# A third buffer for gathered rows, a gather beside each product, and a sum moved behind a mask, in a two-layer graph kernel

## The chip, the cores and the metric

The kernel runs on one core of one Trainium2 chip, as one program with one launch. The metric is the device time of that core in microseconds (us), the median of several runs. Five runs of the kernel before gave 1269.19 us as the median (1265.02 to 1273.97).

A core has engines that run side by side, each through its own list of instructions in order: TensorE (PE in the profile; PEld is its weight load), VectorE (DVE), ScalarE (ACT), GpSimd (POOL) and SyncE (SP), which here only issues DMAs. They wait for each other through semaphores. An instruction that waits holds up all that stand behind it in the list of its engine.

## What is computed

Input are x, 2708 x 256, and a square matrix adj, 2708 x 2708, with about 0.3 % of entries not zero. Layer 0 is a graph layer with LayerNorm; layer 1 is a two-step propagation, with LayerNorm too:

```python
support = adj @ x
x = _layernorm(x + relu(concat([x, support], 1) @ weight + bias))

R = adj + eye(N);  R = R / R.sum(-1, keepdims=True)
Z = 0;  Xf = x;  Xa = x
for n in range(2):
    A = _top_p_attention(Xa, W1, W2, W3)
    Xf = R @ Xf
    Xa = A @ Xa
    Z = Z + Xf @ U1[n].T + Xa @ U2[n].T
x = _layernorm(x + _layernorm(x + Z))
```

`_top_p_attention` forms softmax(q kT) over all 2708 columns, keeps in each row the largest probabilities until their sum reaches 0.9 (of equal ones the first), sets the others to zero and divides by the sum of what is kept.

## The kernel before

**Blocks.** The 2708 rows are NB = 22 blocks of 128 rows (the last, EDGE, has 20). A block of attention is a 128 x 2708 tile of exponentials `e`; four such tiles `es` (a fifth in step 2) are in use in turn.

**Three stages.** Layer 0 runs first and keeps x1 in SBUF. Step 1 of the attention (the loop at L931 over t) follows, then step 2 (the loop at L1311 over `per`). The text calls one turn of the latter a pass.

**R is kept sparse.** For each block m of R, layer 0 names the columns of adj that have any entry in these rows: at most 896, as CC = 7 chunks of CW = 128. During step 1, `adj_gather` (L377) fetches those columns' blocks of adj, and `adj_store` packs them in DRAM (`adjc_d`, and the diagonal block in `own_d`). A product of R with a vector block is then 8 *units*, each one matmul of 128 x 256: seven over the gathered chunks (k = 0 to 6) and one over the block's own rows (k = 7). The row numbers are in `ix`.

**Gathered rows of y.** The right side of unit k is 128 rows of `yf_d` (first half, s = 0) or `v_d` (second half, s = 1), gathered by an indirect DMA that GpSimd issues: `y_load` (L742), seven for a product (L746). They land in `yg`, which has two slots, `m % 2`; each slot has eight parts, the eighth for the block's own rows, which SP loads (L762). The rows of `v_d` are completed by the first half's results (`r_out` stores to `v_d`, L806), so the gathers of the second half can't start before the last product of the first half is stored.

**Order of R's units.** `r_units(n)` (L765) issues the next n units. With the first unit of product m it calls `r_load(s, m + 1)`: SP loads the packed blocks of R (`a_load`, one of three buffers `adj`), GpSimd issues the seven gathers, SP loads the own rows. The last unit of a product starts a load of what is to be added (`v_load` or `za_load`), and puts `r_out` into `later`, which VectorE runs two turns of g on. The first two products' gathers are issued at the end of step 1 (`y_at`, L928).

The table `units` (L1294) says how many units a pass has: 16 (`first`) before the loop, then 8 and 8 in passes 0 and 1, 18 in each of passes 2 to 9, none in pass 10 and 16 in each of passes 11 to 21. A pass spreads them over six turns g.

**A pass of step 2.** Pass `per` works on several blocks at once: the exponentials of block per + 2 (ScalarE L871, L875, as logits from TensorE L534 come in, the last third at g = 3), two tries for the threshold of block per + 1 (ScalarE L1002, L1005, with small instructions L1008 to L1018 behind them), the search of candidates of block per (VectorE L1059, L1066), the end of the search and the mask of block per - 1 (VectorE: L1075 to L1119, mask L1124), and the product of block per - 2 with ya (TensorE transposes L561, ScalarE copies L563, TensorE L590). TensorE's order within a turn g is written out by hand. VectorE's is a generator, `vector_slots` (L1146), of which each g runs one slot; the last slot runs marks 2 and 3, `begin_search` of the block per + 2 between them (L879 to L884: the sum of the three parts of the exponentials' sum, its reciprocal, its negative and the first level), and then the mask.

**LayerNorm at the end.** `Final` and `final_slot` (L1260): rows that have all their parts (`ready`) are normalised in the next passes. `middle` runs at g = 0: ScalarE writes to one of four `spares` (L1228), GpSimd multiplies and adds (L1243, L1244), and VectorE takes the second statistics (L1218) at g = 4 of the same pass.

**Room.** `yg`, the spares and `x1_edge` (the last block's rows, for step 1) share one tile, `y_room`. `c.u1`, the matrices U1, is read by `u1_project` (L673) before step 1's loop, and in `general_path`, which runs only if a flag says that the fast path's assumptions failed.

Of the kernel before, what the change touches and what calls it, by code (L numbers as in the profile page):

```python
# [20 lines left out]
P = 128  # L21
# [18 lines left out]
ML = 16  # L40
CW, CC = 128, 7
EARLY = 12
AT = 96
# [19 lines left out]
def gnn_two_layer_kernel(ctx: ExitStack, tc: tile.TileContext, N, xT_d, x_d, adj_d, w0_d, b0_d,  # L63
# [24 lines left out]
    nc = tc.nc  # L88
    D = x_d.shape[1]
    DA = w1_d.shape[1]  # L90
    NB = (N + P - 1) // P
    DC = D // P
# [13 lines left out]

    c = Common()
    c.N, c.D, c.DA, c.NB, c.DC, c.KH, c.CHS, c.rows = N, D, DA, NB, DC, KH, CHS, rows
    c.adj_d, c.out_d = adj_d, out_d
# [21 lines left out]
    NF = 6 * NB + 4  # L131
# [28 lines left out]
def fast_path(ctx, tc, c, flags, fint, xT_d, x_d, w0_d, b0_d, w1_d, w2_d, w3_d, u1_d, u2_d, g_d, b_d):  # L160
# [351 lines left out]
    assert not weights  # L512
    lists.end()
    y_room = big.tile([P, DC * N], FP, tag="Y", name="yg")
    YW = 2 * (CC + 1) * D
    yg = y_room[:, :YW].rearrange("p (s c d) -> p s c d", s=2, d=D)
    spares = [y_room[:, YW + D * i:YW + D * (i + 1)] for i in range(4)]
    x1_edge = y_room[:, YW + 4 * D:YW + 5 * D]
    lists = Lists(ML, NB, flags[:, NF - 2:], yg[:, 1].rearrange("p c d -> p (c d)"))
    lists.turn()  # L520

    NL = len(KPS) // 2
# [216 lines left out]
    later = [[], []]  # L739
    ready = []  # L740

    def y_load(s, m):  # L742
        y = yg[:, m % 2]
        rows_d = (c.yf_d, c.v_d)[s].rearrange("p k d -> (p k) d")
        for i in range(CC):
            nc.gpsimd.indirect_dma_start(out=y[:CW, i, :], out_offset=None, in_=rows_d,  # L746
                                         in_offset=bass.IndirectOffsetOnAxis(ap=ix[:CW, m, i:i + 1], axis=0))
        y_in[s, m] = y

    def a_load(m):  # L750
        a = adjp.tile([P, KH, P], FP, tag="adj", name="adj_t")
        nc.sync.dma_start(out=a[:CW, :CC, :].rearrange("p c i -> p (c i)"), in_=c.adjc_d[m])
        nc.sync.dma_start(out=a[:rows(m), CC, :], in_=c.own_d[m, :rows(m), :])
        a_in[m] = a

    def r_load(s, m):
        if m not in a_in:
            a_load(m)
        if (s, m) not in y_in:
            y_load(s, m)  # L760
        y = y_in.pop((s, m))
        nc.sync.dma_start(out=y[:rows(m), CC, :], in_=(c.yf_d, c.v_d)[s][:rows(m), m, :])  # L762
        r_in[s, m] = a_in.pop(m), y

    def r_units(n):  # L765
        for _ in range(n):
            s, m = r_queue[0]
            p = rows(m)
            if not r_now:
                r_now[:] = [ps_misc(), 0]  # L770
                if m + 1 < NB:
                    r_load(s, m + 1)
            acc, k = r_now
            a, y = r_in[s, m]
            kw = CW if k < CC else p
            nc.tensor.matmul(acc[:p, :D], lhsT=a[:kw, k, :p], rhs=y[:kw, k, :], start=k == 0, stop=k == CC)  # L776
# [24 lines left out]
    def r_out(s, m, acc, base):  # L801
        p = rows(m)
        if s == 0:
            nc.vector.scalar_tensor_tensor(base[:p], acc[:p, :D], rinv[:p, m:m + 1], base[:p],
                                           op0=ALU.mult, op1=ALU.add)
            nc.sync.dma_start(out=c.v_d[:p, m, :], in_=base[:p])  # L806
            if m == NB - 1:
                r_load(1, 0)
        else:
            arrive(m, base, acc, rinv[:p, m:m + 1])  # L810

# [107 lines left out]
    for t in range(n_u, NB):  # L919
        u1_project(t)  # L920
    extract1(2)
    nc.vector.memset(x1_edge, 0.0)
    nc.vector.tensor_copy(x1_edge[AT:AT + rows(EDGE)], x1[:rows(EDGE), EDGE, :])
    ends = None

    at = {(m // 2, 3 * (m % 2) + 1): m for m in range(4)}
    at.update({(m - 2, 3): m for m in range(4, NB)})
    y_at = {(NB - 2, 2): 0, (NB - 2, 5): 1}  # L928
    stores = []
    blocks = {}  # L930
    for t in range(NB):  # L931
# [214 lines left out]
    def vector_slots(a, b, begin):  # L1146
# [47 lines left out]
        yield  # L1194

    new, finals, done = [], [], []
# [215 lines left out]
def general_path(ctx, tc, c):  # L1412
# [13 lines left out]
    work = ctx.enter_context(tc.tile_pool(name="gwork", bufs=2))  # L1426
    small = ctx.enter_context(tc.tile_pool(name="gsmall", bufs=4))
    ps = ctx.enter_context(tc.tile_pool(name="gps", bufs=2, space=PSUM))

    def ps_lg():  # L1430
        return ps.tile([P, CH], FP, tag="lg", name="lg")
# [339 lines left out]
```

## Time and profile before

| | us |
|---|---|
| median of five runs | 1269.19 |
| the profiled execution | 1266.74 |
| its span, first to last instruction | 1265.0 |
| first unit of R (L776) starts | 722.8 |
| last gather of yf_d starts | 938.7 |
| first gather of v_d starts | 953.9 |
| last gather of v_d starts | 1217.9 |

| engine | busy us | share of the span |
|---|---|---|
| TensorE | 1192.0 | 94 % |
| TensorE's weight loads | 901.2 | 71 % |
| VectorE | 971.5 | 77 % |
| ScalarE | 734.7 | 58 % |
| GpSimd | 634.0 | 50 % |

How to read it: the median is over several executions, and the profile is of one of them, so sums over the profile are made against 1265.0 us. Matmul records overlap (the next starts before the last ends), so a share of 94 % for TensorE doesn't mean that it is at its peak. A float32 matmul leaves two records (704 for the 352 units of R). A pass of step 2 is read most easily from the starts of the mask, L1124. In rows of a timeline, a bracket tells the idle time of the engine before the instruction and what ended it.

### The profile page before, as it was taken

How to read it: one execution, taken by the hardware profiler on the slowest of the kernel's cores; microseconds unless marked ns; L12 is line 12 of the kernel's file. 1: busy time of each engine (PE TensorE's matmuls, PEld its weight loads, DVE VectorE, ACT ScalarE, POOL GpSimd, SP SyncE). 2: the span in 40 equal slices, each digit the busy share in tenths (PEclk: the TensorE clock that was granted, in tenths of full speed). 3: DMA queues.
4: the chain of work that ended last, by engine and by line, in shares of the span. 5: the costliest groups of instructions: out<-in, count | busy, mean ns of one | idle time of the engine just before them, and what ended most of it. 6: DMA issues, size and time to landing. Idle time of an engine off the chain costs nothing.

```text
span 1265.0 us, 18701 instructions
## 1 busy us (share of the span) xinstructions
PE 1192.0 (94%) x5772; PEld 901.2 (71%) x5772; DVE 971.5 (77%) x3254; ACT 734.7 (58%) x1299; POOL 634.0 (50%) x596
## 2 busy tenths in 40 slices
PE   8999999999899999999998969999998999999884
PEld 6888878863477777777776737777766777777663
DVE  2455545875999998988851399887788999999886
ACT  2000110135566665666665499878879999999821
POOL 1000000004545542677765087787756888888850
PEclk9999999999899999999999989999999999999997
DMA  7475445434222220233333155656654645655551
GB/s 200 152 209 177 152 142 175 135 106 126 88 66 82 74 72 10 60 98 101 89 80 98 58 173 179 185 180 187 179 118 127 198 142 172 198 152 167 165 116 30
DMA packets 104248, 164.92 MB, mean 130 GB/s; under 512 B 20162, under 2 KB 76870, under 8 KB 104138
## 3 DMA queue, kind: packets, MB, share of 16 engines
q1 hardware_dynamic: 77852, 107.57, 26.5%
q0 software_dynamic: 20544, 51.17, 15.7%
q10 hardware_dynamic: 5742, 4.89, 1.4%
q8 instruction: 48, 0.79, 0.3%
q14 instruction: 62, 0.51, 0.1%
HBM read 129.66 MB, written 33.90 MB: 129 GB/s over the span
## 4 chain that ended last, share of the span: by engine, by line
PE 37%; DVE 8%; ACT 6%; DMA 6%; issue 2%; POOL 2%; POOLq 0%; ACTq 0%
PE acc L590 17%; PE misc L776 7%; PE lg L534 5%; PE tr L561 4%; DMA yg<-v_d,ix 3%; DMA yg<-yf_d,ix 3%; DVE e L1124 2%; PE acc L698 2%; ACT e L1002 2%; DVE w L1119 1%; ACT e L1005 1%; ACT e L871 1%; PE misc L726 1%; POOL yg L746 1%; DVE cand L1066 1%
## 5 line engine op out<-in xcount | busy, mean ns | idle before, releaser
L563 ACT COPY wT<-tr 128x512 f32<-128x512 f32 (+2 forms) x258 | 136.4, 536 | 203.7 <-PE tr L561 203.7
L746 POOL DMA_INDIRECT yg<-v_d,ix x154 | 194.1, 1261 | 59.7 <-issue 25.0
L590 PE MATMUL acc<-ya,wT 128*128 128x256 f32 x924 | 222.9, 383 | 0.0
L590 PE MATMUL acc<-x,wT 128*128 128x256 f32 x882 | 218.8, 389 | 0.0
L746 POOL DMA_INDIRECT yg<-yf_d,ix x154 | 189.2, 1229 | 48.3 <-issue 25.6
L274 PE MATMUL acc<-y,adj_t 128*128 128x257 f32 x924 | 204.4, 380 | 0.0
L776 PE MATMUL misc<-yg,adj_t 128*128 128x256 f32 (+1 forms) x704 | 186.2, 395 | 18.5 <-DMA yg<-yf_d,ix 7.7
L590 PEld LDWEIGHTS acc<-x,wT 128*128 128x128 f32 x882 | 160.3, 191 | 58.9 <-issue 25.5
L590 PEld LDWEIGHTS acc<-ya,wT 128*128 128x128 f32 x924 | 172.3, 191 | 37.9 <-issue 16.7
L274 PEld LDWEIGHTS acc<-y,adj_t 128*128 128x128 f32 x924 | 173.9, 190 | 26.6 <-issue 1.9
L384 POOL DMA_INDIRECT adj_t<-in_adj,ix x154 | 163.7, 1063 | 51.6 <-issue 43.9
L776 PEld LDWEIGHTS misc<-yg,adj_t 128*128 128x128 f32 (+1 forms) x704 | 122.4, 189 | 69.4 <-issue 20.6
L534 PE MATMUL lg<-k,q 64*128 64x512 f32 (+3 forms) x528 | 137.1, 596 | 20.8 <-ACT e L871 7.4
L561 PE MATMUL tr<-ident,e 128*128 128x128 f32 (+1 forms) x946 | 145.1, 272 | 6.3 <-ACT wT L563 4.6
L561 PEld LDWEIGHTS tr<-ident,e 128*128 128x128 f32 (+1 forms) x946 | 117.4, 141 | 39.3 <-ACT wT L563 8.6
L351 POOL DMA_DIRECT2D part_d<-e x1 | 0.6, 573 | 272.6 <-DVE e L350 272.6
L1002 ACT ACTIVATE e<-e,st 128x2708 f32<-128x2708 f32 (+1 forms) x43 | 113.6, 2641 | 0.1
L1005 ACT ACTIVATE e<-e,st 128x2708 f32<-128x2708 f32 (+1 forms) x42 | 111.0, 2642 | 0.1
L462 ACT COPY x1T<-tr 128x256 f32<-128x256 f32 (+1 forms) x22 | 8.0, 364 | 174.6 <-PE tr L461 174.6
L596 DVE MAX8 cand<-e 128x8 f32<-128x170 f32 (+1 forms) x352 | 86.2, 316 | 14.7 <-ACT e L541 14.5
L1066 DVE MAX8 cand<-w 128x8 f32<-128x170 f32 (+1 forms) x352 | 94.1, 321 | 0.0
L534 PEld LDWEIGHTS lg<-k,q 64*128 64x128 f32 (+1 forms) x528 | 39.1, 182 | 52.6 <-issue 20.2
(247 smaller groups left out, 1744.3 us busy)
## 6 DMA issues: line engine op xcount, KB each, us to landing
adj_t<-in_adj SPq DMA_DIRECT2D x42, 704.0 KB
adj_t<-adjc_d SPq DMA_DIRECT2D x44, 448.0 KB
adjc_d<-adj_t SPq DMA_DIRECT2D x22, 256.0 KB
base<-za_d SPq DMA_DIRECT2D x40, 128.0 KB
adjc_d<-adj_t SPq DMA_DIRECT2D x22, 192.0 KB
xt<-in_x ACTq DMA_DIRECT2D x21, 128.0 KB
x_d<-x SPq DMA_DIRECT2D x21, 128.0 KB
x1b_d<-xb SPq DMA_DIRECT2D x21, 128.0 KB
```

The lines of the kernel that those rows point to most:

```text
L274: nc.tensor.matmul(acc[:p, :n], lhsT=halves[k // KH][:, k % KH, :p], rhs=y[:, k, :n], start=k == 0, stop=stop and k == NB - 1)
L384: nc.gpsimd.indirect_dma_start(out=a[:CW, i, :], out_offset=None, in_=adj_rows, in_offset=bass.IndirectOffsetOnAxis(ap=ix[:CW, m, i:i + 1] ...
L534: nc.tensor.matmul(lg[:p, h, at:at + b - a], lhsT=q[o, t * P:t * P + p], rhs=keys[s][o, i, :b - a], start=True, stop=True)
L561: nc.tensor.transpose(tr[:, k % 4, :p], columns(e[:p], k), ident[:p, :p])
L563: nc.scalar.copy(wT[:, :len(ks), :p], tr[:, :len(ks), :p])
L590: nc.tensor.matmul(acc[:p, :D], lhsT=wT[:, k % 4, :p], rhs=part_y(y, k), start=k == 0, stop=k == NB - 1)
L596: nc.vector.max(dst[:p, i * 8:(i + 1) * 8], src[:p, i * step:i * step + w])
L746: nc.gpsimd.indirect_dma_start(out=y[:CW, i, :], out_offset=None, in_=rows_d, in_offset=bass.IndirectOffsetOnAxis(ap=ix[:CW, m, i:i + 1], ...
L776: nc.tensor.matmul(acc[:p, :D], lhsT=a[:kw, k, :p], rhs=y[:kw, k, :], start=k == 0, stop=k == CC)
L1002: nc.scalar.activation(scr[:b.p, :N], e, AF.Relu, bias=b.nz, scale=b.l[k], accum_out=b.relu)
L1005: nc.scalar.activation(scr[:b.p, :N], e, AF.Sign, bias=b.nz, scale=b.l[k], accum_out=b.sign)
L1066: nc.vector.max(b.cand[:p, 8 * i:8 * i + 8], low[:p, SEG2 * i:SEG2 * (i + 1)])
```

## The change

- `yg` has three slots of seven parts. The own rows go to two free parts of the tile that holds R's blocks.
- With the first unit of product m, `r_load` is called for m + 2. It no longer issues the gathers but puts them in a list, `to_gather`; each unit issues one of them ahead of its matmul.
- The gathers of the first three products are issued at the end of step 1, and so are the loads of R's blocks for the first two.
- The units: 24 ahead of the loop (`first`), 8 and 16 in passes 0 and 1, 16 in each of passes 2 to 9; none in pass 10 and 16 in passes 11 to 21 as before.
- When the first half is stored, the loads and gathers of the second half's first two products are issued, all fourteen gathers in a row.
- The spares and `x1_edge` move to `c.u1`, and `x1_edge` is written inside step 1's loop at t = 0. `general_path` loads U1 again.
- In the last slot of `vector_slots` the mask comes right after marks 2 and 3, and `begin_search` behind it.

```diff
@@ fast_path @@
-    YW = 2 * (CC + 1) * D
-    yg = y_room[:, :YW].rearrange("p (s c d) -> p s c d", s=2, d=D)
-    spares = [y_room[:, YW + D * i:YW + D * (i + 1)] for i in range(4)]
-    x1_edge = y_room[:, YW + 4 * D:YW + 5 * D]
+    YW = CC * D
+    yg = y_room[:, :3 * YW].rearrange("p (s c d) -> p s c d", s=3, d=D)
+    idle = [c.u1[:, j, i, :] for j in range(DC) for i in range(2)]
+    spares = list(idle)
+    x1_edge = idle[0]
...
+    def y_rows(s, m, i):
+        rows_d = (c.yf_d, c.v_d)[s].rearrange("p k d -> (p k) d")
+        nc.gpsimd.indirect_dma_start(out=yg[:CW, m % 3, i, :], out_offset=None, in_=rows_d,
+                                     in_offset=bass.IndirectOffsetOnAxis(ap=ix[:CW, m, i:i + 1], axis=0))
+
     def y_load(s, m):
-        y = yg[:, m % 2]
-        rows_d = (c.yf_d, c.v_d)[s].rearrange("p k d -> (p k) d")
         for i in range(CC):
-            nc.gpsimd.indirect_dma_start(out=y[:CW, i, :], out_offset=None, in_=rows_d,
-                                         in_offset=bass.IndirectOffsetOnAxis(ap=ix[:CW, m, i:i + 1], axis=0))
-        y_in[s, m] = y
+            y_rows(s, m, i)
+        y_in[s, m] = yg[:, m % 3]
...
-    def r_load(s, m):
+    to_gather = []
+
+    def r_load(s, m, by_unit=False):
         if m not in a_in:
             a_load(m)
         if (s, m) not in y_in:
-            y_load(s, m)
-        y = y_in.pop((s, m))
-        nc.sync.dma_start(out=y[:rows(m), CC, :], in_=(c.yf_d, c.v_d)[s][:rows(m), m, :])
-        r_in[s, m] = a_in.pop(m), y
+            if by_unit:
+                to_gather.extend((s, m, i) for i in range(CC))
+                y_in[s, m] = yg[:, m % 3]
+            else:
+                y_load(s, m)
+        a, y = a_in.pop(m), y_in.pop((s, m))
+        own = a[:, CC + 1:CC + 1 + D // P, :].rearrange("p c i -> p (c i)")
+        nc.sync.dma_start(out=own[:rows(m)], in_=(c.yf_d, c.v_d)[s][:rows(m), m, :])
+        r_in[s, m] = a, y, own
...
             if not r_now:
                 r_now[:] = [ps_misc(), 0]
-                if m + 1 < NB:
-                    r_load(s, m + 1)
+                if m + 2 < NB:
+                    r_load(s, m + 2, True)
+            if to_gather:
+                y_rows(*to_gather.pop(0))
...
             if m == NB - 1:
                 r_load(1, 0)
+                r_load(1, 1)
...
-    y_at = {(NB - 2, 2): 0, (NB - 2, 5): 1}
+    y_at = {(NB - 3, 5): 0, (NB - 2, 3): 1, (NB - 1, 1): 2}
...
+        if t == 0:
+            nc.vector.memset(x1_edge, 0.0)
+            nc.vector.tensor_copy(x1_edge[AT:AT + rows(EDGE)], x1[:rows(EDGE), EDGE, :])
...
-            if (t, g) == (NB - 1, 2):
-                a_load(0)
+            if t == NB - 1 and 1 < g < 4:
+                a_load(g - 2)
...
     r_load(0, 0)
+    r_load(0, 1)
...
@@ vector_slots @@
-        for i in (2, 3):
-            if b:
-                mark(b, i)
-            if begin:
-                next(begin)
+        if b:
+            mark(b, 2)
+            mark(b, 3)
+            mask(b)
         if begin:
             run_all(begin)
-        if b:
-            mask(b)
         yield
...
-    first = 2 * (CC + 1)
-    units = {0: CC + 1, 1: CC + 1}
+    first = 3 * (CC + 1)
+    units = {0: CC + 1, 1: 2 * (CC + 1)}
```

More of the change, by code (lines that the diff above doesn't have):

```diff
@@ L108, in gnn_two_layer_kernel @@
     c.N, c.D, c.DA, c.NB, c.DC, c.KH, c.CHS, c.rows = N, D, DA, NB, DC, KH, CHS, rows
-    c.adj_d, c.out_d = adj_d, out_d
+    c.adj_d, c.out_d, c.u1_d = adj_d, out_d, u1_d
     c.x1_d = dram.tile([N, D], FP, name="x1_d")
@@ L514, in fast_path @@
     y_room = big.tile([P, DC * N], FP, tag="Y", name="yg")
-    YW = 2 * (CC + 1) * D
-    yg = y_room[:, :YW].rearrange("p (s c d) -> p s c d", s=2, d=D)
-    spares = [y_room[:, YW + D * i:YW + D * (i + 1)] for i in range(4)]
-    x1_edge = y_room[:, YW + 4 * D:YW + 5 * D]
-    lists = Lists(ML, NB, flags[:, NF - 2:], yg[:, 1].rearrange("p c d -> p (c d)"))
+    YW = CC * D
[3 more added lines that the diff above has]
+    x1_edge = idle[0]
+    lists = Lists(ML, NB, flags[:, NF - 2:], y_room[:, YW:])
     lists.turn()
@@ L770, in r_units @@
                 r_now[:] = [ps_misc(), 0]
-                if m + 1 < NB:
-                    r_load(s, m + 1)
+                if m + 2 < NB:
+                    r_load(s, m + 2, True)
+            if to_gather:
+                y_rows(*to_gather.pop(0))
             acc, k = r_now
-            a, y = r_in[s, m]
+            a, y, own = r_in[s, m]
             kw = CW if k < CC else p
-            nc.tensor.matmul(acc[:p, :D], lhsT=a[:kw, k, :p], rhs=y[:kw, k, :], start=k == 0, stop=k == CC)
+            nc.tensor.matmul(acc[:p, :D], lhsT=a[:kw, k, :p], rhs=y[:kw, k, :] if k < CC else own[:p],
+                             start=k == 0, stop=k == CC)
             r_now[1] += 1
@@ L921, in fast_path @@
     extract1(2)
-    nc.vector.memset(x1_edge, 0.0)
-    nc.vector.tensor_copy(x1_edge[AT:AT + rows(EDGE)], x1[:rows(EDGE), EDGE, :])
     ends = None
@@ L1428, in general_path @@
     ps = ctx.enter_context(tc.tile_pool(name="gps", bufs=2, space=PSUM))
+    for s in range(2):
+        nc.sync.dma_start(out=u1[:, :, s, :], in_=c.u1_d[s].rearrange("(c p) e -> p c e", p=P))
     def ps_lg():
```

## The prediction

> **What bounds the kernel now.** I read the page first, then busy time by stretches one pass of step 2's loop long, then the timelines of GpSimd, VectorE and TensorE inside passes, and last the table of waits. The page's part 1 suggests TensorE and nothing else:
>
> ```profile
> PE 1192.0 (94%) x5772; PEld 901.2 (71%) x5772; DVE 971.5 (77%) x3254; ACT 734.7 (58%) x1299; POOL 634.0 (50%) x596
> ```
>
> The share hides that in step 2 (from about 722 us on) GpSimd never stops. In its timeline a gather (L746) takes 0.95 us and the next starts 0.30 us later, so 1.25 us each. Twice a pass one is stretched:
>
> ```profile
> 869.62 3.71 POOL L746 DMA_INDIRECT yg<-yf_d,ix  x1 [0.30 <-PE misc L776]
> 873.63 0.95 POOL L746 DMA_INDIRECT yg<-yf_d,ix  x1 [0.31 <-PE misc L776]
> 874.88 0.95 POOL L746 DMA_INDIRECT yg<-yf_d,ix  x1 [0.30 <-issue]
> 876.13 2.90 POOL L746 DMA_INDIRECT yg<-yf_d,ix  x1 [0.30 <-PE misc L776]
> ...
> 938.66 0.94 POOL L746 DMA_INDIRECT yg<-yf_d,ix  x1 [0.30 <-issue]
> 953.92 0.94 POOL L746 DMA_INDIRECT yg<-v_d,ix  x1 [14.32 <-PE lg L534]
> ```
>
> ```profile
> 869.46 3.04 DVE L1124 SCALAR_TENSOR_TENSOR e<-w,st,e 128x2720 f32<-128x2720 f32 x1
> 875.17 3.03 DVE L1059 SCALAR_TENSOR_TENSOR w<-e,st 128x2720 f32<-128x2720 f32 x1
> ```
>
> The stretched gathers are those that meet VectorE's two 128x2720 passes, the mask (L1124) and L1059. The 0.30 between gathers is there whatever is named behind it, so it is price, not waiting. Added up over the GpSimd timeline from 723.8 to 939.6: 140 gathers x 1.248 = 174.7, plus 41.1 excess of 18 stretched ones (2.28 each) = 215.8 us, the whole stretch. From 953.9 to 1221.9: 154 x 1.248 = 192.2, 48.2 for 22 stretched ones, nine groups of LayerNorm products (L1243, L1244) of some 3.0 = 27, together 267.4 of 268.0. Only two places are idle: 14.3 us between the two halves, and 685.9 to 722, before step 2.
>
> Now one pass at a time (columns: stretch, length, then busy us and instructions of PE, PEld, DVE, ACT, POOL, clock, DMA):
>
> ```profile
> 779.00:801.00 22.00, 22.00 (x111) 17.21 (x110) 19.86 (x70) 19.85 (x33) 17.74 (x15) 1.00 0.60 181
> 801.00:824.00 23.00, 23.00 (x114) 17.80 (x113) 19.89 (x69) 19.74 (x33) 18.43 (x16) 1.00 0.60 172
> 872.50:897.20 24.70, 24.47 (x118) 18.49 (x117) 20.02 (x71) 19.93 (x34) 19.82 (x17) 1.00 0.60 183
> 969.40:990.00 20.60, 20.50 (x102) 16.00 (x103) 19.56 (x68) 19.81 (x33) 16.64 (x14) 1.00 0.51 154
> 990.00:1012.30 22.30, 22.30 (x112) 17.49 (x111) 20.91 (x75) 19.91 (x34) 18.03 (x15) 1.00 0.57 177
> ```
>
> A pass of the first half holds 18 units of R, so 15.75 gathers: 15.75 x 1.248 + 2 x 2.28 = 24.2 us. From one start of L1124 to the next, the passes take 22.0, 23.2, 23.4, 25.1, 24.7, 24.2, 23.8: at first TensorE is packed and GpSimd falls behind, then TensorE waits for gathers. The last two rows, passes of 16 units, give TensorE's own price: 214 records in 42.9 us, 0.2005 us each. A 16-unit pass has 44 + 22 + 12 + 32 = 110 records: 22.05 us.
>
> **The change, part by part.**
>
> *One product moves ahead of step 2.* Seven gathers go into GpSimd's idle time at 685.9 to 722 and cost 7 x 1.25 = 8.75 us there, of 36. If that cover were gone they would cost what they save. Of the 20 products with gathers left in the first half, 19 remain. Passes 2 to 9 fall from 18 units to 16, so 14 gathers: 14 x 1.248 + 4.57 = 22.04 us on GpSimd and 22.05 on TensorE. VectorE (about 20.0 busy) and ScalarE (19.9) have room. The two bounds are equal, and 2 us below the present passes.
>
> *The sixteen units that go forward* are 16 x 0.432 = 6.9 us of TensorE ahead of pass 0 and in pass 1 (four matmuls, recorded as eight, take 1.73 us in the chain's L590 rows). This part of the timeline has room, as its waits show:
>
> ```profile
> 736.75 1.13 PE L776 MATMUL misc<-yg,adj_t 128*128 128x256 f32 x2 [2.38 <-DMA yg<-yf_d,ix]
> 752.88 2.08 PE L534 MATMUL lg<-k,q 64*128 64x512 f32 x4 [5.47 <-ACT e L871]
> 758.35 1.04 PE L561 MATMUL tr<-ident,e 128*128 128x128 f32 x8
> ```
>
> but not for nothing. Pass 1 now ends with product 5, whose seventh gather is GpSimd's 21st from 723.8 on. The 21st starts now at 755.69; a gather lands some 3.6 us after its start (1209.14 to 1212.82 in the chain). The first two units of pass 2 need the 22nd and 23rd, so the first transposes of pass 2 go at 758.19 + 3.6 + 0.5 = 762.3 instead of 758.35: 4 us late. VectorE is as late: r_out of product 2 now stands with those of products 0 and 1 ahead of the candidates (L1066, now at 730.88), and product 2 ends only at 730.6 + 8 x 0.432 = 734.1, 3.3 us later. Both delays meet at pass 2, so they count once. Bounds: 0 (all in waits) and +6.9 (all on the path); I take +4.
>
> *Sum to the end of the first half.* First transposes of pass 10 now: 948.9 (TensorE's timeline). After, by TensorE: 762.3 + 8 x 22.05 = 938.7, or -10.2. By GpSimd: 755.7 + 8 x 22.04 + 3.6 for landing + 0.9 for the last two units = 936.5 against 946.9 now, -10.4. Two engines with one price wait for each other now and then. Bounds for that: 0, and 8 x 1.1 (the 23.2 us of the present second pass) = 8.8; I take 1.2, since the 16-unit passes of the second half run packed. **About -9.**
>
> *A third slot, one gather with each unit.* In the second half GpSimd has 154 gathers and the same products as before, in nearly the same order, and no gap to fill: 0. Its start moves with the end of the first half. With a lead of two products, units 0 and 1 of a pass put two gathers ahead of its LayerNorm products: 2 x 1.25 = 2.5 us later. Behind them waits VectorE's L1218, and behind that everything on VectorE:
>
> ```profile
> DVE bulk L879 <- ACT e L871: 21.8, 12, 3.0
> ...
> DVE bst L1218 <- POOL yg L1244: 10.7, 9, 2.7
> ```
>
> ```profile
> SPq L762 <- PE misc L776: 99.3, 24, 16.4
> ```
>
> (The table of waits from 750 to 1235 us, and SP's own from 700 to 1240: total us, times, longest.) Until about 1100 L1218 comes 2 to 5 us after them; after that it waits already, because GpSimd is late. A shift of 2.5 us there happens once, and ends with the last pass, which has no gathers ahead of its products. Bounds 0 and 2.5; I take 0. On SP the load of R's blocks now waits for the product before, but the own-row load in the same call (the L762 row) waits for the same product today; what is behind it (za, x1b, v) is needed a third of a pass or more later. 0, and if a load of some 2 us showed at each of 44 products, it would be up to 44 x 2. I see no such row, so 0.
>
> *The sum over parts behind the mask.* L879 no longer stands ahead of mark 3 and the mask; 21.8 us of waits in 12 places vanish there. Who is late next: L1039, right after the mask, needs ScalarE's L1018. At 894 that ends at 896.8, and L1039 ran at 897.7, so VectorE wins 0.9 of 3 us. TensorE waited for the mask 1.7 us in three places altogether. In the first half the gain sinks in the equal bounds above. In pass 10 (no units; ScalarE busy 19.9 of 24.2) it might start the second half's gathers earlier. Bounds 0 and -3; I take 0. Moved x1_edge, u1's room and the loads at step 1's end: two small VectorE instructions for two, a load on SP without a queue behind it: 0, within 0.5 either way.
>
> Total: -9 of the profiled 1265.0 us span. That execution took 1266.74 and the median of the runs is 1269.19; I take the difference off the median: **1260 us**, its own range 1254 to 1264.
>
> One rule speaks against this. The Trainium skill, page "SBUF — State Buffer", section "SBUF: two separate sides", says that VectorE and GpSimd share a port pair as an exclusive lock held for the whole instruction, also by a VectorE instruction with two SBUF inputs, and that the loser blocks fully. By it each pass loses 2 x 3.04 = 6.1 us, a 14-gather pass costs 23.6, and 8 passes give back 12 us: no gain at all. The row says 2.28, not 3.04, and by the rule today's passes would be 25.7, where 24.2 is measured late in the half; I go by the row.
>
> **Rivals.**
> - *Passes stay near 23.2* (17 in 100): TensorE, VectorE and GpSimd hinder each other as in the pass at 801. 762.3 + 8 x 23.2 = 947.9, -1: 1268. For: two bounds within 0.01 us. Against: 22.05 over two packed passes.
> - *More is won* (11): the 4 us of start-up vanish in waits and the second half starts 3 us earlier by the mask: -9 - 4 - 3 = -16, 1253. For: TensorE is busy 19.7 us of the 31.6 from 726.8. Against: the 21st gather's time.
> - *The late LayerNorm products* (10), slower: VectorE is the bound of the second half (22.5 to 23.6 busy of 23.3 to 23.9 at 1012 to 1106). If it waits 2.5 us more in each of nine passes, instead of once, it costs 22.5 - 9 = +13: 1282. It decides from where L1218 waits in every pass from the first (1029) on; the present slack of 2 to 5 us there, and GpSimd's 25 us a pass against VectorE's 22, speak against it.
> - *It doesn't do what it says* (7): the gather of two products ahead waits for its slot, so GpSimd gets no earlier and only order changes: 0, 1269. Against: the slot was last read by the product before.
>
> The likeliest has 55. **Range** 1250 to 1271: it leaves out most of the slower case and the best of the gains. This kernel can tell 0.5% (6.3 us) from no change. Faster by more: 52 of the likeliest's 55 and the 11, 0.63; within: 3, 17, 5 of the 7, 0.25; slower: 10 and 2, 0.12.
>
> **What would show it.** Right: gathers of the first half number 133 after 723, with 14 per pass; masks 22 to 22.5 us apart up to pass 9; first v_d gather near 945; first transposes of pass 2 near 762; L879 without waits, L1039 with some; second half unchanged in length. Wrong: GpSimd idle in passes 2 to 9 while TensorE has gaps, L1218 waiting from 1029 on, or the step 1 end moved.

## The result and the profile after

The changed kernel takes 1265.73 us (median of 29 runs, 1262.59 to 1267.84) against 1268.31 for the kernel before (51 runs, 1264.23 to 1273.97): ratio 0.9978, interval [0.9971, 0.9985]. That is -2.6 us where -9 was forecast: 1265.7 lies within the range, but the clear gain isn't there. Of all the runs below one, the fifth of e15, took 6530.5 us; the ratios leave it out.

The profiled execution took 1267.87 us, its span 1266.1. It lies 1.1 us over the profiled one of before, because it enters step 2 late: the first unit of R starts at 726.77 and not at 722.82. In the profiles of eleven experiments whose kernels are alike up to there it lies between 723.2 and 727.5. Step 2 alone, from there to the end of the span, takes 539.3 us (before 542.1); that is -2.8, close to the medians' -2.6, so the late start is in good part this execution's (whether all of it is stays open, see the end). From here on times in step 2 are counted **from the first unit of R**.

The page's first part hides the matter as it did before:

```profile
PE 1199.0 (95%) x5772; PEld 908.7 (72%) x5772; DVE 974.5 (77%) x3254; ACT 735.0 (58%) x1299; POOL 639.3 (50%) x596
```

GpSimd's timeline in pass 4 (start, length, engine, line, operation), and VectorE's two long passes beside it:

```profile
829.71 2.59 POOL L745 DMA_INDIRECT yg<-yf_d,ix  x1 [0.30 <-PE misc L788]
832.61 0.94 POOL L745 DMA_INDIRECT yg<-yf_d,ix  x1 [0.30 <-PE lg L535]
...
836.35 3.52 POOL L745 DMA_INDIRECT yg<-yf_d,ix  x1 [0.30 <-PE misc L788]
...
937.13 0.94 POOL L745 DMA_INDIRECT yg<-yf_d,ix  x1 [0.30 <-PE misc L788]
953.41 0.94 POOL L745 DMA_INDIRECT yg<-v_d,ix  x1 [15.34 <-PE lg L535]
```

```profile
828.43 3.05 DVE L1140 SCALAR_TENSOR_TENSOR e<-w,st,e 128x2720 f32<-128x2720 f32 x1
...
836.03 3.03 DVE L1075 SCALAR_TENSOR_TENSOR w<-e,st 128x2720 f32<-128x2720 f32 x1
```

L1140 is the mask (L1124 before), L1075 the next block's pass (L1059 before). From mask to L1075 it is 7.60 us here, where the prediction's rows of before have 5.71.

Busy times by pass (stretch, length, PE, PEld, DVE, ACT, POOL, clock, DMA; stretches run nearly from mask to mask), a pass of the first half and two of the second:

```profile
829.50:851.70 22.20, 22.20 (x111) 17.38 (x111) 19.98 (x70) 19.48 (x33) 17.73 (x15) 1.00 0.57 177
...
1127.20:1152.80 25.60, 23.42 (x109) 17.87 (x108) 22.26 (x78) 22.29 (x40) 21.31 (x19) 0.93 0.55 165
1152.80:1178.50 25.70, 23.18 (x114) 17.66 (x112) 22.29 (x80) 22.29 (x40) 21.41 (x19) 1.00 0.50 152
```

The first half came out near the forecast: 23.8, 23.0 and 22.6 us for passes 2 to 4 and 22.3 from pass 5 on (forecast 22.05), with TensorE packed. But passes of the second half take 25.7 us, in which TensorE and VectorE each have over 2 us idle. The start-up, answering the three TensorE rows of before, and the waits of VectorE and TensorE from 750 to 1235 us (the last two lines: TensorE's for the mask, changed and before):

```profile
743.02 1.22 PE L788 MATMUL misc<-yg,adj_t 128*128 128x256 f32 x2 [2.14 <-DMA yg<-yf_d,ix]
...
759.99 2.08 PE L535 MATMUL lg<-k,q 64*128 64x512 f32 x4 [0.34 <-ACT e L885]
...
767.53 1.92 PE L562 MATMUL tr<-ident,e 128*128 128x128 f32 x8
```

```profile
DVE bst L1231 <- POOL u L1257: 13.7, 11, 2.2
DVE st L1055 <- ACT st L1034: 9.4, 11, 1.8
```

```profile
PE tr L562 <- DVE e L1140: 12.1, 4, 4.7
...
PE tr L561 <- DVE e L1124: 1.7, 3, 1.0
```

The waits of the sum over parts (21.8 us before) are gone, and L1055, the second of the steps behind the mask, waits for ScalarE instead. New is that TensorE waits 12.1 us for the mask (1.7 before).

Laid side by side, the starts of the mask after the first unit (us, from VectorE's timelines; "before + mask" and "no mask part" are the first two experiments, e1 and e2). The length of pass n is from here on the time from the mask of pass n to the next.

| mask of pass | before | changed | before + mask | no mask part |
|---|---|---|---|---|
| 1 | 21.8 | 26.5 | 21.7 | 26.5 |
| 11 | 264.2 | 257.0 | 260.4 | 258.4 |
| 16 | 380.6 | 374.8 | 378.0 | 375.4 |
| 20 | 476.6 | 477.1 | 480.4 | 472.6 |
| 21 | 501.4 | 499.5 | 505.2 | 495.0 |

The change leads by 7.2 us at pass 11, by 5.8 at pass 16, and has lost all of it at pass 20. Both kernels with the sum behind the mask lose time between passes 16 and 20 against their partners without it: 6.4 us (e1 against before) and 5.1 us (changed against e2).

### The profile page after: what moved, and what is told of

The parts are those of the page before. It is cut to its first block, busy times and chain, and to the rows that moved or that the text cites. A ratio compares the mean times of both kernels' runs of the same rounds, so it can differ in the third digit from the quotient of the medians.

```text
span 1266.1 us, 18670 instructions
## 1 busy us (share of the span) xinstructions
PE 1199.0 (95%) x5772; PEld 908.7 (72%) x5772; DVE 974.5 (77%) x3254; ACT 735.0 (58%) x1299; POOL 639.3 (50%) x596
## 4 chain that ended last, share of the span: by engine, by line
PE 45%; ACT 6%; DMA 4%; POOL 2%; DVE 2%; issue 2%; POOLq 0%; ACTq 0%
PE acc L591 21%; PE misc L788 9%; PE lg L535 6%; PE tr L562 5%; DMA yg<-yf_d,ix 3%; PE acc L699 2%; POOL yg L745 1%; ACT e L1021 1%; PE misc L727 1%; DMA yg<-v_d,ix 1%; ACT e L885 1%; DVE e L1140 1%; ACT e L1018 1%; ACT wT L564 1%; ACT u L1241 1%
## 5 line engine op out<-in xcount | busy, mean ns | idle before, releaser
L745 POOL DMA_INDIRECT yg<-v_d,ix x154 | 197.4, 1282 | 60.7 <-issue 24.8
L591 PE MATMUL acc<-ya,wT 128*128 128x256 f32 x924 | 225.6, 386 | 0.0
L788 PE MATMUL misc<-yg,adj_t 128*128 128x256 f32 (+1 forms) x616 | 166.2, 398 | 11.2 <-DMA yg<-yf_d,ix 8.0
L562 PE MATMUL tr<-ident,e 128*128 128x128 f32 (+1 forms) x946 | 147.8, 276 | 16.8 <-DVE e L1140 12.1
L788 PEld LDWEIGHTS misc<-yg,adj_t 128*128 128x128 f32 (+1 forms) x616 | 108.6, 192 | 55.4 <-issue 17.4
L1018 ACT ACTIVATE e<-e,st 128x2708 f32<-128x2708 f32 (+1 forms) x43 | 113.5, 2641 | 0.1
L1135 DVE MATCH_REPLACE8 w<-part,e 128x680 f32<-128x680 f32 (+1 forms) x88 | 74.2, 850 | 0.0
```

Of the source, the lines that this page charges most:

```text
L562: nc.tensor.transpose(tr[:, k % 4, :p], columns(e[:p], k), ident[:p, :p])
L591: nc.tensor.matmul(acc[:p, :D], lhsT=wT[:, k % 4, :p], rhs=part_y(y, k), start=k == 0, stop=k == NB - 1)
L745: nc.gpsimd.indirect_dma_start(out=yg[:CW, m % 3, i, :], out_offset=None, in_=rows_d, in_offset=bass.IndirectOffsetOnAxis(ap=ix[:CW, m, i: ...
L1018: nc.scalar.activation(scr[:b.p, :N], e, AF.Relu, bias=b.nz, scale=b.l[k], accum_out=b.relu)
```

## The experiments

**Each half of the change alone.** e1 is the kernel before with nothing but the new order in the last slot; e2 the changed kernel with the old order there.

```diff
 e1 (on before), taken back in e2 (on the changed kernel); lines joined
-        for i in (2, 3):
-            if b: mark(b, i)
-            if begin: next(begin)
-        if begin: run_all(begin)
-        if b: mask(b)
+        if b: mark(b, 2); mark(b, 3); mask(b)
+        if begin: run_all(begin)
```

> The kernel before with the mask ahead of begin_search, and nothing else of the change. Theory G (GpSimd's chain of gathers sets the end of both halves): that chain isn't touched, 1267.5 to 1269 against 1268.3, mask waits gone all the same. Rival M (the mask carries the 2.6 us that were won): 1265 to 1266.

> The changed kernel with begin_search between the marks again. G: as the changed kernel, 1265 to 1266.5. M: 1268 or more.

e1: 1271.25 us, ratio 1.0031 [1.0018, 1.0044], outside what either theory allowed: the order alone makes the kernel slower. e2: 1259.59, ratio 0.9933 [0.9919, 0.9948], below what either theory allowed; the rest of the change is worth 8.5 us by the ratio, 7.5 by the medians. (A second time, as e13 below: 0.9937.)

**The table of units, and the end of the first half.** e3 keeps two products ahead of the loop as before; e4 hands out the last product's output (and with it the second half's gathers) one slot earlier.

```diff
 e3
-    first = 3 * (CC + 1)
-    units = {0: CC + 1, 1: 2 * (CC + 1)}
+    first = 2 * (CC + 1)
+    units = {0: CC + 1, 1: CC + 1}
 e4
-    later[1].append(lambda ...: r_out(s, m, acc, base))
+    later[(s, m) != (0, NB - 1)].append(lambda ...: r_out(s, m, acc, base))
```

> The changed kernel with the old table of units (16 ahead of the loop, 8 and 8, then 18 a pass): same gathers in the same order on GpSimd, TensorE has 1.0 to 1.2 us more to do in each of passes 2 to 9 and 6.9 us less before them. G: within 1 us of the changed kernel, 1265 to 1267, last gather of the first half within 1 us as well. Rival T (TensorE's 22.5 us a pass is what is left of the gain): passes of 23.4 or more, 1270 to 1273.

> The changed kernel with r_out of the last product of the first half one turn earlier, ahead of VectorE's 3.04 us pass L1075. G: the first gather of v_d starts some 3 us earlier and the end comes 3 us earlier, 1262 to 1263.5. T, or VectorE as the bound of the second half: the gathers start earlier and the end stays, 1265 to 1266.5.

e3: 1262.56, ratio 0.9957 [0.9944, 0.9970], under both theories' ranges. The mask of pass 1 is back at 22.6, the passes of the first half take some 23.1 us, and the second half's first gather starts 223.8 us after the first unit instead of 226.6. The start-up price that I forecast is real, and not worth paying: the third buffer gives GpSimd its lead without it. e4: 1263.67, ratio 0.9965 [0.9951, 0.9978], between the two ranges. Those gathers start at 224.4, but the mask of pass 21 stands at 499.7 (499.5 in the changed kernel): what the second half gets earlier doesn't reach the end.

**Where the 6 us go.** In the changed kernel, GpSimd around the mask of pass 17 and VectorE beside it:

```profile
1124.10 0.73 POOL L1257 TENSOR_TENSOR u<-u,x1b 128x256 f32<-128x256 f32 x1
1124.97 1.01 POOL L745 DMA_INDIRECT yg<-v_d,ix  x1
1126.28 0.95 POOL L745 DMA_INDIRECT yg<-v_d,ix  x1 [0.30 <-issue]
1127.53 3.52 POOL L745 DMA_INDIRECT yg<-v_d,ix  x1 [0.30 <-PE acc L591]
...
1133.86 3.56 POOL L745 DMA_INDIRECT yg<-v_d,ix  x1 [0.30 <-issue]
```

```profile
1124.86 0.43 DVE L1231 BATCH_NORM_STATS2 bst<-u 128x6 f32<-128x256 f32 x1 [0.85 <-POOL u L1257]
...
1127.18 3.05 DVE L1140 SCALAR_TENSOR_TENSOR e<-w,st,e 128x2720 f32<-128x2720 f32 x1
...
1133.56 3.05 DVE L1075 SCALAR_TENSOR_TENSOR w<-e,st 128x2720 f32<-128x2720 f32 x1
```

And in e2, whose line numbers are three higher behind L1140:

```profile
1119.95 0.73 POOL L1260 TENSOR_TENSOR u<-u,x1b 128x256 f32<-128x256 f32 x1
1120.82 1.01 POOL L745 DMA_INDIRECT yg<-v_d,ix  x1
1122.13 0.95 POOL L745 DMA_INDIRECT yg<-v_d,ix  x1 [0.30 <-issue]
1123.38 0.95 POOL L745 DMA_INDIRECT yg<-v_d,ix  x1 [0.30 <-PE misc L788]
1124.64 2.58 POOL L745 DMA_INDIRECT yg<-v_d,ix  x1 [0.30 <-issue]
...
1128.78 0.95 POOL L745 DMA_INDIRECT yg<-v_d,ix  x1 [0.30 <-DMA yg<-v_d,ix]
1130.03 2.97 POOL L745 DMA_INDIRECT yg<-v_d,ix  x1 [0.31 <-PE misc L788]
```

```profile
1120.71 0.43 DVE L1234 BATCH_NORM_STATS2 bst<-u 128x6 f32<-128x256 f32 x1 [0.85 <-POOL u L1260]
...
1123.36 3.04 DVE L1140 SCALAR_TENSOR_TENSOR e<-w,st,e 128x2720 f32<-128x2720 f32 x1
...
1129.13 3.04 DVE L1075 SCALAR_TENSOR_TENSOR w<-e,st 128x2720 f32<-128x2720 f32 x1
```

The kernel before, at the mask of its pass 17, has the same phases as e2:

```profile
1126.33 0.96 POOL L746 DMA_INDIRECT yg<-v_d,ix  x1 [0.30 <-issue]
1127.60 2.59 POOL L746 DMA_INDIRECT yg<-v_d,ix  x1 [0.30 <-PE misc L776]
...
1132.99 2.96 POOL L746 DMA_INDIRECT yg<-v_d,ix  x1 [0.30 <-issue]
```

```profile
1126.33 3.04 DVE L1124 SCALAR_TENSOR_TENSOR e<-w,st,e 128x2720 f32<-128x2720 f32 x1
...
1132.09 3.04 DVE L1059 SCALAR_TENSOR_TENSOR w<-e,st 128x2720 f32<-128x2720 f32 x1
```

Read them as a race. Both kernels are held in step by the LayerNorm products: VectorE's statistics wait for the last one, two marks follow, then the mask. GpSimd meanwhile sends gathers every 1.25 us. In e2 the sum's four instructions stand ahead of the mask, among the two marks and behind them, so the mask starts 2.65 us after the statistics; the third gather, 0.02 us after the mask's start, still gets through in 0.95, and the next, 1.28 after it, lasts 2.58. In the changed kernel the mask starts 2.32 us after the statistics, the third gather comes 0.35 us too late and lasts 3.52. The lengths follow one line: a gather that starts d after the start of a long pass ends 3.86 us after that start, so it lasts 3.86 - d (1.28 and 2.58; 0.35 and 3.52). Over all eighteen profiles the 702 held gathers end 3.85 to 3.91 us after it. The four instructions now behind the mask do the same once more: they widen mask to L1075 from 5.77 to 6.38 us, and the gather that meets L1075 comes 0.30 after its start and lasts 3.56, not 2.97 (at 0.90). Together 0.93 + 0.60 = 1.53 us a pass; 25.65 - 24.13 is 1.52.

Call this theory Q. Before I had both halves of it, I tested the second alone (theory P). e5 shortens the way from mask to L1075 in the changed kernel; e6 lengthens it in e2 with four useless instructions. Beside them, e7 joins e2, e3 and e4, and e8 is e2 with a product's gathers all at once.

```diff
 e5 (on the changed kernel)
-        run_all(turns((part_of_it(order, 7) if b else None, 1), (levels, 1)))
+        run_all(turns((part_of_it(order, 4) if b else None, 1), (levels, 1)))
 e6 (on e2)
+    def idle4(b):
+        x = small.tile([P, 4], FP, tag="idle4", name="idle4", bufs=1)
+        nc.vector.tensor_reduce(x[:b.p, 0:1], b.all[:b.p, :NL], AX.X, ALU.add)
+        nc.vector.reciprocal(x[:b.p, 1:2], x[:b.p, 0:1])
+        nc.vector.tensor_scalar(x[:b.p, 2:3], x[:b.p, 0:1], -1.0, None, op0=ALU.mult)
+        nc.vector.tensor_scalar(x[:b.p, 3:4], x[:b.p, 2:3], x[:b.p, 0:1], x[:b.p, 1:2], op0=ALU.mult, op1=ALU.mult)
...
             mask(b)
+            if begin:
+                idle4(b)
 e8 (on e2)
-            if to_gather:
+            while to_gather:
                 y_rows(*to_gather.pop(0))
```

> The changed kernel, but with only four (not seven) of the next block's ordering steps in VectorE's first slot, so that the time between the mask and the next pass over all exponentials (L1075) falls back from 3.33 to about 2.6 us in the second half (before: 2.73), while the sum over exponentials' parts stays behind the mask. Theory P (the gap between VectorE's two long passes decides how long the gather that meets the second one is blocked): passes 16 to 19 take 24.1 us again, not 25.65, the gather that meets L1075 lasts 2.6 to 3.0 us and not 3.56, and the time falls by 4 to 6 us against the changed kernel, to 1259.5-1262. Rival A (the later sum makes ScalarE's search and with it the next pass late): the sum is as late as in the changed kernel, so passes 16 to 19 stay at 25.6 and the time at 1264.5-1267.

> The kernel of e2_no_mask (sum ahead of the mask) with four more small VectorE instructions of no use, copies of the sum's own four, right behind the mask: 0.6 us of VectorE a pass, and the gap between the two long passes grows from 2.73 to about 3.33 us; the sum itself is as early as before. Theory P: passes 16 to 19 go from 24.13 to 25.6 us, the gather that meets L1075 from 2.97 to 3.56, the time rises by 4.5 to 6.5 us over e2 (1264-1266). Rival A (the late sum): nothing but 0.6 us once or in the few passes that VectorE bounds, 1259.5-1261. Rival V (VectorE bounds the passes): 0.6 us in each of 18 passes, +8 to +11 us, with the passes of the first half at 22.9.

> The changed kernel with the sum ahead of the mask as in e2, the old table of units (two products and not three ahead of the first pass) as in e3, and the last product's output ahead of L1075 as in e4. If the three act in different places (e2: passes 16 to 19, -6 us; e3: start-up and first half, -3; e4: between the halves, -1.6 to -3), the sum is 1253-1256. If GpSimd's chain is one chain and swallows the start-up part (it is GpSimd and not TensorE that sets the first half), 1256-1259. If e2's gain depends on the phase that the first half leaves, anything up to 1262.

> The kernel of e2_no_mask with all seven gathers of a product issued together, two products ahead, as far as the third buffer allows, and not one with each unit. If the third buffer alone brings the gain: first v gather about 227 us after the first unit as in e2 (before: 231), and a time within 1.5 us of e2 (1258.5-1261) unless LayerNorm's products wait behind seven gathers. If the spacing matters for the second half (LayerNorm's products up to 8.8 us later in GpSimd's queue, VectorE waiting for them): first half as e2, but the second half 3 to 12 us longer, 1262-1272. If the spacing brought the whole gain: first half as before, 231 us.

e5: 1263.32, ratio 0.9964 [0.9950, 0.9977]; passes 16 to 18 take 25.25 us. The way was only cut to 5.96 us, the gather at L1075 lasts 3.15, but the one at the mask still 3.54. e6: 1265.87, ratio 0.9988 [0.9977, 0.9999]; passes of 24.76, the gather at L1075 3.59, the one at the mask 2.60. Both missed P's 24.1 and 25.6, so P alone fell; each moved one of the two gathers and left the other, which is what led to Q. e6's total fits P's range, but its passes don't. V, by which VectorE's 0.6 us more are paid in every pass, holds in places: passes 4 to 6 take 22.7 to 23.3 us (22.28 in e2), and the 0.63 more of passes 16 to 18 could as well be V's. But passes 8, 10 and 11 are e2's own (22.28, 20.68 and 22.28), and the total stays below V's +8 to +11 over e2. What V can't explain is e9, below.

e7: 1257.59, ratio 0.9925 [0.9909, 0.9942]: not the sum of the three, but within what was allowed for one chain that swallows the start-up part. e8: 1262.77, ratio 0.9962 [0.9946, 0.9977]. Its first half is e2's (first v_d gather at 226.4, e2 227.1, before 231.1), so that gain comes without the spacing. Passes 12 to 19 take 196.3 us in place of 191.9, 2.6 of it in pass 12 alone (26.64 us), where LayerNorm's products stand behind more gathers; pass 20 is 0.8 shorter. One gather with each unit is worth these 3.6 us.

**Useless work that helps.** Q says that the mask comes too early in the changed kernel. So e9 puts the four useless instructions ahead of the mask, and e10 adds e5's shorter way. e11 leaves out LayerNorm's two products on GpSimd, and e12 is e7 with the second of a pass's two LayerNorms on VectorE.

```diff
 e9 (on the changed kernel; e10 has e5's edit too)
             mark(b, 3)
+            if begin:
+                idle4(b)
             mask(b)
 e11 (on e2)
-            nc.gpsimd.tensor_tensor(h[:p], h[:p], c.gb[:p, 0, :], op=ALU.mult)
-            nc.gpsimd.tensor_tensor(h[:p], h[:p], self.x1[:p], op=ALU.add)
 e12 (on e7), in Final.middle
-            if tail:
+            if tail or self.i:
```

> The changed kernel (sum over parts behind the mask) with four small VectorE instructions of no use right ahead of the mask, some 0.5 us of work more a pass. Theory Q (phase: in passes 16 to 19 VectorE starts each turn of the mask when the last LayerNorm product is done, so the time from that product to the mask, 2.68 us in e2 and 2.36 in the changed kernel, decides whether GpSimd's third gather behind the products, which starts 2.69 us after them, gets in at the mask's start or is caught by it; and the gap from mask to L1075 does the same for the next): the mask falls at 2.8 to 2.95 us, the gather caught there is a later one that lasts 2.7-2.85 us and not 3.53, the one caught by L1075 stays at 3.56, passes 16 to 19 take 24.8-25.0 us in place of 25.65: useless work makes the kernel faster there, and the whole by 0 to 4 us (1261.5-1266 against before's 1267.5; the first half may give some back). Rival V (VectorE's work bounds the passes): passes 26.1-26.3 and 1268-1275. Theory P alone (only the gap to L1075 counts): 25.6, time unchanged.

> The kernel of e9 with the shorter way from the mask to L1075 of e5 (four ordering steps ahead of it and not seven): both phases moved back, while the sum stays behind the mask. Theory Q: gather at the mask 2.7-2.85 us, at L1075 3.1-3.2, passes 16 to 19 24.4-24.6 us, the time 2 to 6 us under the changed kernel's (1259.5-1263.5). Rival V: as e9, passes over 25.6 and 1267-1275. Rival A (the later sum itself is the loss): passes 25.2 or more as in e5, time as e5 or longer.

> The kernel of e2_no_mask without GpSimd's two LayerNorm products a block (multiplication by the weights and addition of x1 left out). Theory G (GpSimd's chain of gathers and products sets the second half, and VectorE only waits for it): GpSimd's pass falls from 24.13 by 4 x 0.75 = 3 us to some 21.2, TensorE's 22.1-22.5 sets the passes 12 to 19, 8 x 1.6 = 13 us less: 1245-1250. Rival V (VectorE): passes stay at 23.5-24.2, the time at 1257-1260.

> The kernel of e7_best with the LayerNorm of the second of the two blocks that come up in one pass done by VectorE (two products with the statistics built in, 0.47 us each, as the kernel's last pass does) and only the first by GpSimd. If GpSimd bounds the second half (G): GpSimd's pass falls by 1.5 us, VectorE's grows by some 0.9 of which 1 us is idle now; passes 12 to 19 at 22.6-23.3, the time 4 to 9 us under e7: 1248.5-1253.5. If VectorE is as near the bound (V): no gain or a loss of up to 5 us: 1257-1263.

The totals of these four say nothing about Q. They ran on a chip where the kernel before took 1309.68 us and every one of them was slower than it: 1.0183 [1.0156, 1.0210], 1.0124 [1.0094, 1.0154], 1.0077 [1.0048, 1.0106], 1.0154 [1.0121, 1.0187]. The granted clock of their profiled executions was 0.962 to 0.969; that of the kernel before on this chip was 0.969 to 0.978. In stretches of 50 us, e9's entry into step 2 (columns as above; the clock is the third from the end):

```profile
700.00:750.00 50.00, 41.69 (x194) 26.15 (x195) 8.85 (x21) 15.86 (x41) 7.43 (x8) 0.80 0.20 61
750.00:800.00 50.00, 27.14 (x104) 19.43 (x102) 17.12 (x64) 23.34 (x33) 33.16 (x35) 0.78 0.49 152
```

The passes later on ran at a clock of 1.00 and can be read. e9, caught gathers and long passes from the mask of pass 15 on:

```profile
1148.37 2.60 POOL L745 DMA_INDIRECT yg<-v_d,ix  x1 [0.30 <-issue]
...
1153.78 3.56 POOL L745 DMA_INDIRECT yg<-v_d,ix  x1 [0.30 <-PE misc L788]
...
1173.11 2.59 POOL L745 DMA_INDIRECT yg<-v_d,ix  x1 [0.30 <-issue]
```

```profile
1147.11 3.04 DVE L1147 SCALAR_TENSOR_TENSOR e<-w,st,e 128x2720 f32<-128x2720 f32 x1
...
1153.47 3.05 DVE L1082 SCALAR_TENSOR_TENSOR w<-e,st 128x2720 f32<-128x2720 f32 x1
```

24.73 us from mask to mask (1147.11 to 1171.84) against 25.65, with more work: Q's direction, and 0.07 below its range. V asked for 26.1 to 26.3, and rival A, by which the late sum itself is the loss, for no gain: the sum is as late here. e10: 24.36, also just under the 24.4 to 24.6. In e11 the passes 13 to 18 take 23.2 to 24.2, not 22.1 to 22.5: VectorE, ScalarE and TensorE are busy 46 to 48.5 of 50 us there and GpSimd waits for TensorE. So as the bound of e2's 24.1 GpSimd seems to be only half a microsecond ahead of the others (e2 and e11 ran on different chips), and my theory G was too simple.

**Again, on a chip where before takes 1268.77.** e13 is e2, e14 is e10, e15 is e12, e16 the changed kernel itself.

> The kernel of e2_no_mask once more, on whatever chip this falls to, beside e14 to e16. If the loss by the mask's order is the kernel's own: ratio to before 0.992 to 0.995, as in e2. If the gain of the rest of the change depends on the chip's clock (the chip of e9 to e12 granted 0.962-0.969 and every kernel was slower than before there): on a chip like that 1.008-1.02, on one like e2's 0.992-0.995.

> The kernel of e10 on a chip where before takes about 1267 us. Theory Q (phase), from the passes that e10 showed undisturbed (24.36 us against 25.65 in the changed kernel): 4 to 5 passes x 1.3 = 5 to 6.5 us less than the changed kernel, less up to 3 us for the useless work in the first half: ratio to before 0.993-0.9965. Rival V (VectorE's work): 1.000-1.006.

> The kernel of e12 on a chip where before takes about 1267 us. Its undisturbed passes 13 to 16 in e12 took 23.1 us against 23.5 in e7's same four; passes 17 to 19 in e7 24.1-24.8. If that holds in all: 4 x 0.4 + 3 x 1.2 = 5 us less than e7: ratio to before 0.987-0.990. If TensorE, VectorE and ScalarE set the second half at 23.6 us as e11 without LayerNorm's products suggests: 0 to -3 us against e7, 0.990-0.993.

> The changed kernel as it is, beside e13 to e15 on their chip: ratio to before 0.9971 to 0.9985 if the chip is like the one of the result; if the chip is like that of e9 to e12 (clock 0.96 to 0.97), the same theory that makes e13 slow there makes this one 1.010-1.02.

e13: 1261.01, 0.9937 [0.9919, 0.9956]. e14: 1263.30, 0.9946 [0.9925, 0.9966]. e15: 1252.37, 0.9866 [0.9844, 0.9889], just past the 0.987 it was given. e16: 1264.32, 0.9966 [0.9952, 0.9980], just under its range but within the interval. V's range for e14 is excluded, and Q's holds it. Against e16 its total is only 1.0 us less, within the intervals; its masks show why it can't be much more: from pass 16 to pass 20 it takes 96.8 us and e16 102.4, but by pass 16 the useless work had cost 3.0. That leaves 2.6.

The evidence for Q is the passes, not that total. For passes 16 to 18 (17 and 18 for before), d is how long after the start of a long pass the gather that it catches begins, and the last column but one is 14 gathers x 1.25 + 2.96 for the products (what e2's pass leaves for them) + both excesses (each 3.86 - d - 0.95 = 2.91 - d):

| kernel | mask to L1075, us | d at mask | d at L1075 | sum | measured |
|---|---|---|---|---|---|
| before, e2, e13 | 5.77 | 1.26 | 0.90 | 24.1 | 24.1 to 24.2 |
| e14 | 5.98 | 1.30 | 0.72 | 24.3 | 24.4 |
| e6 | 6.39 | 1.26 | 0.27 | 24.8 | 24.8 |
| e9 | 6.37 | 1.27 | 0.30 | 24.7 | 24.7 to 24.8 |
| e5 | 5.96 | 0.33 | 0.72 | 25.2 | 25.25 |
| changed, e1, e16 | 6.37 | 0.34 | 0.30 | 25.6 | 25.65 |

The 2.96 is taken from e2; the other rows agree with it to 0.1 us. By itself that says only that GpSimd is busy without a break in these passes; that the phase sets their length is what e9 and e14 show, where the passes get shorter with more work on VectorE (e14 and e16 on one chip: 24.4 against 25.7 us).

One thing in Q as I wrote it is not so: in e9 and e14 VectorE no longer waits for LayerNorm's products at all (it is busy 98 of 100 us from 1095 on). The phase at the mask is the favourable one there, but it isn't that wait which sets it. The traces show another hold: small VectorE instructions that run beside the products are stretched. In e9, with two of the products:

```profile
1213.51 0.68 DVE L1134 TENSOR_TENSOR part<-sc,ranks 128x32 f32<-128x32 f32 x1
1214.22 0.77 DVE L1137 TENSOR_SCALAR part<-part,st 128x32 f32<-128x32 f32 x1
```

```profile
1213.41 0.72 POOL L1265 TENSOR_TENSOR u<-u,gb 128x256 f32<-128x256 f32 x1
1214.22 0.73 POOL L1266 TENSOR_TENSOR u<-u,x1b 128x256 f32<-128x256 f32 x1
```

In e2, where the products run later than these two, they take 0.19 and 0.24 us. In pass 17 of e9 four instructions lose some 1.8 us so. Whether this is what keeps the phase isn't shown.

e15 is the best version measured here; its passes 12 to 19 take 185.4 us, e7's 190.1. In two of its windows VectorE and TensorE are both within 0.4 us of full:

```profile
1083.00:1106.00 23.00, 22.61 (x111) 17.15 (x110) 22.65 (x81) 21.61 (x38) 18.21 (x17) 1.00 0.59 184
1106.00:1129.00 23.00, 22.68 (x112) 17.20 (x111) 22.65 (x81) 21.69 (x38) 18.22 (x17) 1.00 0.58 184
```

## Why the prediction was wrong

**The step that failed** is the last edit's: "The sum over parts behind the mask. [...] Bounds 0 and -3; I take 0." By totals it costs 3.3 us (e16 less e13) to 5.7 us (the ratios 0.9978 and 0.9933 of 1268), and alone +4 us (e1). I looked for what waits on the moved instructions and found ScalarE's L1018, rightly: L1055 does wait, and the first half even gains (e1 leads before by 3.8 us at pass 11, 3.0 of them from pass 1). I did not ask what else their place decides. They are 0.3 us ahead of the mask and 0.6 behind it, and with them two long passes slid against GpSimd's row of gathers. The bounds excluded a loss without a reason.

**The price of 2.28 for a caught gather** was the mean over many phases, and right as that: halfway along 2.91 - d with d from 0 to 1.25 is 2.29. In a locked loop no mean is paid. Both catches together cost 3.66 us in e2 and 5.2 in the changed kernel. The SBUF rule of the Trainium skill (page "SBUF — State Buffer", section "SBUF: two separate sides") that the prediction set against it is nearer in kind. By it, whichever of the two starts first has the port pair for the whole instruction, and the prediction made 3.04 us a catch of that. For a gather that starts d after the pass the rule gives a wait of 3.04 - d (an estimate from the rule and the length of the pass), and the traces show 2.91 - d. Where they differ is a gather that has begun: by the rule the pass would wait for it, and here both run (e2 at L1075: the gather of 1128.78 takes 0.95 us, and the pass that starts 0.35 us behind it 3.04).

**"The second half [...] 0"** fails by that loss, and in the other direction at the end: pass 20 holds 10 gathers in e2 and 12 before, since gathers run a product further ahead, and takes 22.36 us, not 24.83. I had priced the lead for the first half only.

**Right**: 133 gathers of the first half in the loop and 14 in most passes; the start-up (first mask 4.7 us later, forecast 4; first transposes of pass 2 at 767.53, less the 3.95 of the late start 763.6, forecast 762.3); L893 without waits and L1055 with some.

**Mis-sized**: the sum to the end of the first half. At the point that the prediction names, the first transposes of pass 10, it forecast -9; from the first unit on, the changed kernel leads by 5.0 us there and e2 by 5.7. The start-up costs 5.2 us by these rows and not 4, and the eight passes take 180.3 us and not 176.4, 22.3 each at best. The comparison of 936.5 with 946.9 set an ideal last unit against a real one (the real one ended at 946.07, that is 942.1 less the late start), and the first gather of v_d, forecast near 945, starts at 953.41, that is 949.5. So the rest of the change agrees with -9 in part by luck: by the masks e2 leads by 5.8 us at pass 11 and by 6.4 at pass 21, 2.4 of which are pass 20's, and its profile's further lead of 2.65 comes behind the last mask, where the last product (L578) took 2.77 us and in before (L577) 4.46. Nothing here tells whether that belongs to the kernel.

**The rivals.** None of them named the phase. "Passes stay near 23.2" is refuted by 22.28; "more is won" by the start-up, which did cost its 4.5 to 5.2 us; "the late LayerNorm products" by e8, where they come later still and cost 3.6 us in all, not 2.5 in each pass; "it doesn't do what it says" by the 133 gathers.

**Open**: whether the moved loads at the end of step 1 cost something: the first unit stands at 725.0 us on the mean of the twelve profiles with the new start, and at 722.8 and 723.2 in the two with the old one, which is too few to tell. Why these kernels lose to the one before on the chip of e9 to e12: in e9 the first unit comes at 754.4, the first mask another 50.7 us later (26.5 in the changed kernel), and pass 10 takes 32.3 us (21.9), but no profile of before was taken there. Why the mask's phase settles at 1.3 us in e9 and e14 without the wait.

## What to carry to other kernels

When two engines get in each other's way and a wait holds them in step, a mean price for the collision can mislead: work out the phase, instruction by instruction from the wait on, for the order before and after. An edit that moves even 0.3 us across a long instruction then has a price for each pass, with either sign. Where a change has a part with a sound sum and a small reordering beside it, measure each alone: here one was worth 7.5 to 8.5 us and the other lost 3.3 to 5.7 of it.

## What the hardware showed unexpectedly

- A gather that starts up to 0.07 us after a 3.04 us VectorE pass goes through in 0.95 us (e2, 0.01 and 0.02 at the mask of passes 16 and 17; e14, 0.05 and 0.06), with one exception: at the mask of pass 19 one that starts 0.01 to 0.02 after it is held for 3.84 in six of the profiles. Every one that starts from 0.08 us on is held until about 3.86 us after the pass's start, whatever its own start: 3.52 at 0.35, 2.96 at 0.90, 2.58 at 1.28.
- Four useless instructions on an engine that is busy 87% of these passes (44.55 of 51.30 us, changed kernel, passes 17 and 18) made them 0.9 us shorter (25.65 to 24.73, e9), and the same four on the other side of the mask made e2's 0.6 us longer (24.13 to 24.76, e6).
- A comparison can change its sign from one chip to another: on three chips e2, e7, e13 and e15 beat the kernel before by 0.6 to 1.3%, while on the chip where 0.962 to 0.969 was granted, the kernel of e15 (as e12) lost 1.5% to it.
